# Coefficient transfers over every second partition, with another layout in DRAM

## The chip, the cores and the metric

The kernel runs on one core of one Trainium2 chip. The metric is device time in microseconds, the median of several executions. A profiled execution of the same kernel gives the profile; times in it count from the first instruction.

## The reference

The input x is an image batch of 4 x 64 channels x 256 x 256 in float32. Four layers follow each other. Layers 0, 2 and 3 are long two-dimensional convolutions whose filter is the outer product of two filters made by a small sine network, plus a scaled residual:

```python
k   = einsum('ijk,imk->ijmk', hx, hy)              # per channel: hx (rows) times hy (columns)
u_f = rfft2(x, s=(512, 512)); k_f = rfft2(k, s=(512, 512)) / 512
out = irfft2(u_f * k_f)[..., :256, :256] + x * bias[:, None, None]
```

Layer 1 works on Haar wavelet coefficients and mixes the channels at each coefficient:

```python
f1  = haar2d(x)
acc = 0
for i in range(2):                                  # two branches
    f4  = einsum('bchw,oc->bohw', f1 * v[i], conv_w[i])
    acc = acc + sign(f4) * relu(abs(f4) - tau[i])
y   = haar2d(acc, inverse=True) + x
```

The convolutions need whole images of one channel, the mixing needs all 64 channels of one coefficient. Between the two the data change their place, by way of DRAM.

## The kernel before

A convolution is two products with Toeplitz matrices (rows, then columns) on TensorE. The Toeplitz tiles tx and ty are read from DRAM with 64 rows of 1 KB a transfer. There are three phases. Phase A does layer 0 and the forward Haar transform, two channels by two images in a step. Phase B mixes the channels and applies the thresholds. Phase C does the inverse Haar transform and layers 2 and 3. The four images are two groups of two. B of group 0 runs beside the second half of A, B of group 1 beside the first half of C: each phase is a list of small pieces, and a helper interleaves two lists. All transfers are issued from the SP queue.

```python
P = 128;  B, C, N = 4, 64, 256
GROUPS = 2;  NB = B // GROUPS;  CI = 4 // NB        # 2 groups, 2 images, 2 channels a step
ROUNDS = C // CI                                    # 32 steps of A (and of C) in a group
STEPS = C                                           # 64 steps of B in a group
W = 2 * N                                           # two rows of coefficients

def coefficients(name):
    return dram.tile([STEPS // 2, 2, C, 2, NB, 2, N], F32, tag=name, name=name)
coef = [coefficients(f"coef{g}") for g in range(GROUPS)]     # A writes, B reads
mixed = [coefficients(f"mixed{g}") for g in range(GROUPS)]   # B writes, C reads
# ... cut ...
def half(r):
    return slice(r * ROW, (r + 1) * ROW)            # ROW = 64 partitions

def all_rows(grp_tile, c0, images):                 # the transfers of A's store and C's load
    n = 2 * NB * W                                  # 2048 elements, 8 KB
    pairs = []
    for e in range(CI):
        at = grp_tile.offset + (c0 + e) * n
        rows = bass.AP(grp_tile.tensor, at, [[2 * C * n, ROW // 2], [C * n, 2], [1, n]])
        pairs.append((rows, images[half(e)].rearrange("p n k -> p (n k)")))
    return pairs
```

In A and C partition e x 64 + m x 2 + q holds channel e of the step's two and pair of rows (m, q). One transfer takes one channel: 64 neighbouring partitions, 8 KB from each, to rows of DRAM that lie C x n = 131072 elements (512 KB) apart. A step has two such transfers.

```python
# phase A
def store(t):
    grp, c0 = t // ROUNDS, t % ROUNDS * CI
    for to, f in all_rows(coef[grp], c0, st[t]["f"]):
        nc.sync.dma_start(to, f)

# phase B: partition q * 64 + c holds channel c
def step_of(ap, s):
    n = NB * W                                      # 1024 elements, 4 KB
    return bass.AP(ap.tensor, ap.offset + (s // 2 * P * 2 + s % 2) * n, [[2 * n, P], [1, n]])

def load(s):
    # ... cut ...
    d["f"] = bp.tile([P, NB, W], F32, tag="ft", name=f"ft_{grp}_{s}", bufs=4)
    nc.sync.dma_start(d["f"].rearrange("p b w -> p (b w)"), step_of(coef[grp], s))
    for name, src in (("v", v), ("tau", taus)):     # 16 rows of DRAM, each to 8 partitions
        t = d[name] = bp.tile([P, 2, W], F32, tag=name, name=f"{name}_{grp}_{s}", bufs=3)
        at = src.offset + s * 4 * W * COPIES
        flat = bass.AP(src.tensor, at, [[2 * W, 2 * COPIES], [0, C // COPIES], [1, 2 * W]])
        nc.sync.dma_start(t.rearrange("p e w -> p (e w)"), flat)

def store(s):
    nc.sync.dma_start(step_of(mixed[grp], s), st[s]["g"].rearrange("p b w -> p (b w)"))

# phase C
def load(t):
    grp, c0 = t // ROUNDS, t % ROUNDS * CI
    st[t]["g"] = big("in", f"g_{t}", 3)
    for rows, g in all_rows(mixed[grp], c0, st[t]["g"]):
        nc.sync.dma_start(g, rows)
```

In B a step is one transfer of 128 partitions in each direction, 4 KB from each, at a pitch of 8 KB in DRAM. A step of B also loads v and tau. It multiplies the mixed channels by v (VectorE, line 602), takes sign and magnitude (ScalarE), subtracts tau and thresholds (VectorE), and adds up in gt (GpSimd). The load of step s+2 is issued in step s.

Of the kernel before, what the change touches and what calls it, by code (L numbers as in the profile page):

```python
# [41 lines left out]
F32 = mybir.dt.float32  # L42
# [5 lines left out]
P = 128  # L48
B, C, N = 4, 64, 256

ROW = 64
# [14 lines left out]
NB = B // GROUPS  # L66
CI = 4 // NB
M = CI * NB

ROUNDS = C // CI  # L70
STEPS = C
# [2 lines left out]
C_PIECES = 4 * BLOCKS + 2  # L74
W = 2 * N


IMAGES = (GROUPS, NB, ROUNDS, CI, BLOCKS, ROW, N)
TO_ROUNDS = (0, 2, 1, 5, 3, 4, 6)
# [10 lines left out]
def conv_haar_kernel(  # L90
    ctx: ExitStack, tc: tile.TileContext, x, zT, w1, wbd, cols, decay, wo_first, decay_first, bias, forward, inverse, wcol, wrow, pack, v, tau, out
):
    nc = tc.nc
# [3 lines left out]
    dram = ctx.enter_context(tc.tile_pool(name="dram", bufs=1, space=DRAM))  # L97


    def coefficients(name):  # L100
        return dram.tile([STEPS // 2, 2, C, 2, NB, 2, N], F32, tag=name, name=name)

    coef = [coefficients(f"coef{g}") for g in range(GROUPS)]
    mixed = [coefficients(f"mixed{g}") for g in range(GROUPS)]
# [22 lines left out]
    def load_x(t):  # L127
        grp, r = divmod(t, ROUNDS)
        xs = big("in", f"x_{t}", 3)

        n = BLOCKS if t == 0 else 2 * M
        for k in range(0, 2 * M, n):
            nc.sync.dma_start(xs[:, k : k + n], x[grp, r, :, k : k + n])
        return xs

    def load_toeplitz(l, t):

        tx = ac.tile([P, CI, N], F32, tag="tx", name=f"tx{l}_{t}", bufs=5)  # L140
        ty = ac.tile([P, N], F32, tag="ty", name=f"ty{l}_{t}", bufs=5)

        def rows(dst, w, e):
            start = (w * C + t % ROUNDS * CI + e) * REPEATS * PERIOD
            src = bass.AP(filt[l].tensor, filt[l].offset + start, [[PERIOD - 4, 16], [PERIOD - 1, 4], [1, N]])
            nc.sync.dma_start(dst, src)

        for e in range(CI):
            for r in range(2):
                rows(tx[r * ROW : (r + 1) * ROW, e, :], 0, e)  # L150
        for e in range(CI):
            rows(ty[e * ROW : (e + 1) * ROW, :], 1, e)
        return tx, ty
# [143 lines left out]
    def half(r):  # L297
        return slice(r * ROW, (r + 1) * ROW)
# [99 lines left out]
    def later(op):  # L398

        waiting.append(op)  # L400
# [8 lines left out]
        for _ in range(count):  # L409
            next(ops, None)  # L410

    def all_rows(grp_tile, c0, images):

        n = 2 * NB * W
        pairs = []
        for e in range(CI):
            at = grp_tile.offset + (c0 + e) * n
            rows = bass.AP(grp_tile.tensor, at, [[2 * C * n, ROW // 2], [C * n, 2], [1, n]])
            pairs.append((rows, images[half(e)].rearrange("p n k -> p (n k)")))
        return pairs  # L420

    def phase_a():


        total = GROUPS * ROUNDS
        st = [dict() for _ in range(total)]

        def filters(t):
            if t < total:
                st[t]["toep"] = first_toep[t] if t < FIRST else load_toeplitz(0, t)  # L430

        def load(t):
            if t < total:
                st[t]["x"] = first_x[t] if t < len(first_x) else load_x(t)

        def rows(t, j):
            s = st[t]
            if j == 0:
                s["y"] = big("t0", f"ay_{t}", 2)
            if j % 2 == 0:  # L440
                s["ps"] = banks(f"a1ps{j}_{t}")
            toeplitz(s["ps"], blocks(s["x"]), filters_x(s["toep"]), j)
            if j % 2:
                for r, ps in enumerate(s["ps"]):
                    y = blocks(s["y"])[:, r, j - 1 : j + 1]
                    later(lambda y=y, ps=ps: nc.scalar.copy(y, ps))

        def columns(t, j):
            s = st[t]
            if j == 0:  # L450
                s["x1"] = big("m0", f"x1_{t}", 2)
            if j % 2 == 0:
                s["ps2"] = banks(f"a2ps{j}_{t}")
            toeplitz(s["ps2"], blocks(s["y"]), filters_y(s["toep"]), j)
            if j % 2:
                for e, ps in enumerate(s["ps2"]):
                    later(lambda e=e, ps=ps: residual(t, e, j, ps))
            if j == BLOCKS - 1:
                s["fw"] = big("m1", f"fw_{t}", 2)
                s["ops"] = forward_free(s["x1"], s["fw"], f"f{t}_")  # L460

        def residual(t, e, j, ps):
            s = st[t]
            c = t % ROUNDS * CI + e
            to, old = (blocks(s[name])[:, e, j - 1 : j + 1] for name in ("x1", "x"))
            nc.vector.scalar_tensor_tensor(to, old, bias_sb[:, c : c + 1], ps, ALU.mult, ALU.add)  # L466

        def product(t, bp):
            s = st[t]
            if bp == 0:  # L470

                s["f"] = big("out", f"f_{t}", 2)
            two = banks(f"a3ps{bp}_{t}")
            fw = blocks(s["fw"])
            haar(two, lambda r, c: fw[half(r), c, 2 * bp : 2 * bp + 2], forward_sb)
            for b, ps in enumerate(two):
                f = s["f"][:, 4 * bp + 2 * b : 4 * bp + 2 * b + 2]
                copy = nc.vector.tensor_copy if b and t < ROUNDS else nc.scalar.copy
                later(lambda f=f, ps=ps, copy=copy: copy(f, ps))  # L479

        def store(t):
            grp, c0 = t // ROUNDS, t % ROUNDS * CI
            for to, f in all_rows(coef[grp], c0, st[t]["f"]):
                nc.sync.dma_start(to, f)
            st[t].clear()

        def piece(t, j):
            flush()
            if j == 0:
                if t == 0:  # L490
                    filters(0)
                    filters(1)
                    load(0)
                    load(1)
                    spread(0, 0)
                filters(t + 2)
            if j < BLOCKS:
                if t < total:
                    rows(t, j)
                if t > 1:  # L500
                    run(st[t - 2]["ops"], 3)
            elif j < 2 * BLOCKS:
                if 0 < t <= total:
                    columns(t - 1, j - BLOCKS)
                if j == BLOCKS and t > 2:
                    store(t - 3)
            else:
                if t > 1:
                    product(t - 2, j - 2 * BLOCKS)
                if 0 < t <= total:  # L510
                    run(st[t - 1]["ops"], 2)
                if j == 2 * BLOCKS + 1:
                    load(t + 2)

        pieces = [lambda t=t, j=j: piece(t, j) for t in range(total) for j in range(A_PIECES)]

        last = [lambda: [piece(total, j) for j in range(BLOCKS + 1)]]
        last += [lambda j=j: piece(total, j) for j in range(BLOCKS + 1, A_PIECES)]
        t = total - 1
        end = [lambda: (flush(), run(st[t]["ops"], 16), store(t - 1))]  # L520
        end += [lambda bp=bp: (flush(), product(t, bp)) for bp in range(2)]
        end.append(lambda: (flush(), store(t)))
        return pieces, last, end

    def phase_b(grp):
# [3 lines left out]
        st = [dict() for _ in range(STEPS)]  # L529
        un = [dict() for _ in range(units)]  # L530
        pieces = []

        def step_of(ap, s):
            n = NB * W
            return bass.AP(ap.tensor, ap.offset + (s // 2 * P * 2 + s % 2) * n, [[2 * n, P], [1, n]])

        def load(s):
            if s >= STEPS:
                return
            d = st[s]  # L540
            d["f"] = bp.tile([P, NB, W], F32, tag="ft", name=f"ft_{grp}_{s}", bufs=4)
            nc.sync.dma_start(d["f"].rearrange("p b w -> p (b w)"), step_of(coef[grp], s))
            for name, src in (("v", v), ("tau", taus)):
                t = d[name] = bp.tile([P, 2, W], F32, tag=name, name=f"{name}_{grp}_{s}", bufs=3)

# [3 lines that stand above are left out]
# [84 lines left out]
            un[u].clear()  # L633

        def store(s):
            nc.sync.dma_start(step_of(mixed[grp], s), st[s]["g"].rearrange("p b w -> p (b w)"))
            st[s].clear()

        def piece(u, j):
# [41 lines left out]
    def phase_c():  # L681
# [4 lines left out]
        st = [dict() for _ in range(total)]  # L686

        def load(t):
            if t >= total:
                return  # L690
            grp, c0 = t // ROUNDS, t % ROUNDS * CI
            st[t]["g"] = big("in", f"g_{t}", 3)
            for rows, g in all_rows(mixed[grp], c0, st[t]["g"]):
                nc.sync.dma_start(g, rows)

        def filters(t, l):
# [258 lines left out]
```

## Time and profile before

| what | value |
|---|---|
| time, median of 3 | 2965.0 us (2959.24 to 2973.0) |
| span of the profiled execution | 2974.9 us |
| TensorE matmul, weight load | 2459.2 us (83%), 1979.5 us (67%) |
| VectorE, ScalarE, GpSimd | 1583.0 us (53%), 1434.8 us (48%), 1946.2 us (65%) |
| moved by DMA | 636.23 MB, mean 214 GB/s |
| coef<-f, ft<-coef, mixed<-gt, g<-mixed | 128 transfers of 512 KB each |
| from issue to landing, median, in that order | 6.3, 11.1, 11.8, 8.8 us |
| v<-in_v, tau<-taus | 128 transfers of 512 KB each, 12.4 and 12.9 us |

How to read it: a share is an average over stages that have different limits, so the prediction takes the stages one by one. An arrow reads "written from": coef<-f is A's store, ft<-coef is B's load, mixed<-gt is B's store, g<-mixed is C's load, out<-o is the result. The span is also given in 40 equal slices with one digit each, the busy share in tenths. The DMA digit is the mean busy share of the core's 16 DMA engines, and GB/s is what they moved.

### The profile page before, as it was taken

To read this page: it belongs to the slowest core of one execution; us is meant where nothing else is said; L and a number is where in the kernel's file an instruction comes from. 1 tells how busy PE (TensorE), PEld (TensorE's weight loads), DVE (VectorE), ACT (ScalarE), POOL (GpSimd) and SP (SyncE) were. 2 spreads that over 40 slices of the span, in tenths; PEclk is the share of its full clock that TensorE was granted. 3 is DMA by queue.
4 is the path that set the end of the run, shared out by engine and by line. 5 is a ranking of instruction groups with operands and counts; after the bars stand their busy time and mean duration, and the time that the engine had idled before them with its cause. 6 is when DMAs were issued, how large, how long until landed. Compare 5 with 4: busy or idle time off the path is not lost.

```text
span 2974.9 us, 119229 instructions
## 1 busy us (share of the span) xinstructions
PE 2459.2 (83%) x53276; PEld 1979.5 (67%) x53276; DVE 1583.0 (53%) x1779; ACT 1434.8 (48%) x2361; POOL 1946.2 (65%) x2422
## 2 busy tenths in 40 slices
PE   6998887677777767768888888888879999999999
PEld 5777775444445445556767766666658887888888
DVE  2443335677777777446666666666652333333333
ACT  1222224566666666346666566666644333343332
POOL 2777766878778877647776776776755545555551
PEclk9999998888788888889999999999999999999999
DMA  5878888899999999677988898888856455454542
GB/s 164 229 213 234 236 244 229 233 270 293 284 267 290 287 280 290 172 194 221 253 243 241 245 249 242 240 242 236 243 167 161 121 141 136 130 146 122 152 126 92
DMA packets 219192, 636.23 MB, mean 214 GB/s; under 512 B 34983, under 2 KB 117576, under 8 KB 186169
## 3 DMA queue, kind: packets, MB, share of 16 engines
q1 hardware_dynamic: 218680, 628.61, 75.7%
q8 instruction: 419, 6.86, 1.0%
q14 instruction: 93, 0.75, 0.1%
HBM read 413.12 MB, written 215.35 MB: 211 GB/s over the span
## 4 chain that ended last, share of the span: by engine, by line
PE 48%; DMA 16%; issue 8%; DVE 6%; POOL 5%; ACT 4%; SPq 1%; DVEq 0%; ACTq 0%; POOLq 0%
PE c1c L304 10%; PE c1r L304 9%; PE c2c L304 9%; PE c2r L304 8%; PE f L587 4%; DMA ft<-coef 4%; DMA v<-in_v 4%; PE c0ps L316 3%; DMA mixed<-gt 2%; DVE x L602 2%; DMA x<-in_x 2%; PE a2ps L304 1%; POOL fw L352 1%; DMA tau<-taus 1%; PE a1ps L304 1%
## 5 line engine op out<-in xcount | busy, mean ns | idle before, releaser
L389 POOL TENSOR_TENSOR i<-i,g 128x16 f32<-128x16 f32 x744 | 393.9, 549 | 591.4 <-ACT g L372 572.3
L602 DVE TENSOR_TENSOR x<-f,v 128x1024 f32<-128x1024 f32 x256 | 312.6, 1221 | 344.1 <-PE f L587 275.9
L587 PE MATMUL f<-ft,mix 64*64 64x512 f32 x2048 | 357.1, 682 | 166.8 <-DMA ft<-coef 130.4
L606 ACT ACTIVATE m<-x 128x1024 f32<-128x1024 f32 x256 | 271.2, 1059 | 343.7 <-DVE x L602 256.1
L304 PEld LDWEIGHTS a1ps<-tx,x 64*64 64x64 f32 x8192 | 334.1, 143 | 134.2 <-ACT f L479 54.8
L304 PE MATMUL a1ps<-tx,x 64*64 64x192 f32 (+3 forms) x8192 | 367.9, 317 | 46.5 <-ACT f L479 23.4
L304 PE MATMUL c1r<-tx,z 64*64 64x192 f32 (+3 forms) x8192 | 337.4, 308 | 60.2 <-issue 60.1
L304 PEld LDWEIGHTS c1r<-tx,z 64*64 64x64 f32 x8192 | 313.5, 139 | 88.8 <-issue 69.4
L304 PE MATMUL c2r<-tx,cy 64*64 64x256 f32 (+3 forms) x8192 | 329.9, 303 | 50.4 <-issue 39.9
L304 PEld LDWEIGHTS c1c<-ty,ch 64*64 64x64 f32 x8192 | 313.5, 135 | 86.9 <-ACT z L723 41.5
L304 PEld LDWEIGHTS a2ps<-ty,ay 64*64 64x64 f32 x8192 | 311.1, 139 | 90.4 <-issue 51.4
L304 PE MATMUL a2ps<-ty,ay 64*64 64x128 f32 (+3 forms) x8192 | 343.2, 309 | 29.1 <-issue 21.9
L610 ACT ACTIVATE a<-x 128x1024 f32<-128x1024 f32 x256 | 264.2, 1032 | 211.5 <-DVE m L616 210.4
L304 PE MATMUL c2c<-ty,ch 64*64 64x128 f32 (+3 forms) x8192 | 332.5, 303 | 40.3 <-issue 37.1
L304 PE MATMUL c1c<-ty,ch 64*64 64x256 f32 (+3 forms) x8192 | 341.9, 302 | 26.2 <-issue 19.9
L304 PEld LDWEIGHTS c2r<-tx,cy 64*64 64x64 f32 x8192 | 309.4, 136 | 80.5 <-issue 53.5
L304 PEld LDWEIGHTS c2c<-ty,ch 64*64 64x64 f32 x8192 | 311.1, 136 | 65.9 <-issue 48.7
L613 DVE TENSOR_TENSOR a<-a,tau 128x1024 f32<-128x1024 f32 x256 | 313.9, 1226 | 41.2 <-ACT a L610 41.1
L735 ACT COPY ch<-c1r 128x512 f32<-128x512 f32 x256 | 137.2, 587 | 393.0 <-PE c1r L304 392.7
L466 DVE SCALAR_TENSOR_TENSOR x<-x,bias_sb,a2ps 128x512 f32<-128x512 f32 x256 | 179.6, 743 | 272.7 <-PE a2ps L304 232.9
L616 DVE SCALAR_TENSOR_TENSOR m<-a,m 128x1024 f32<-128x1024 f32 x256 | 313.2, 1223 | 21.7
L628 POOL TENSOR_TENSOR gt<-gt,m 128x1024 f32<-128x1024 f32 x128 | 302.9, 2366 | 19.9 <-DVE m L616 16.1
(71 smaller groups left out, 3228.5 us busy)
## 6 DMA issues: line engine op xcount, KB each, us to landing
coef<-f SPq DMA_DIRECT2D x128, 512.0 KB, 6.3
ft<-coef SPq DMA_DIRECT2D x128, 512.0 KB, 11.1
v<-in_v SPq DMA_DIRECT2D x128, 512.0 KB, 12.4
tau<-taus SPq DMA_DIRECT2D x128, 512.0 KB, 12.9
mixed<-gt SPq DMA_DIRECT2D x128, 512.0 KB, 11.8
g<-mixed SPq DMA_DIRECT2D x128, 512.0 KB, 8.8
x<-in_x SPq DMA_DIRECT2D x63, 1024.0 KB, 10.8
out<-o SPq DMA_DIRECT2D x63, 1024.0 KB, 4.9
```

What stands on the lines that cost most here:

```text
L304: nc.tensor.matmul(ps[r][half(c), j % 2, k * ROW :], data[half(r), c, k, bass.ts(j, ROW)], t(r, c)[:, : N - k * ROW], start=k == 0, stop=k ...
L316: nc.tensor.matmul(ps[r][half(c)].rearrange("p h k -> p (h k)"), matrix[half(r)], pairs(r, c).rearrange("p h k -> p (h k)"), start=True, s ...
L389: engine.tensor_tensor(to, s, d, op)
L466: nc.vector.scalar_tensor_tensor(to, old, bias_sb[:, c : c + 1], ps, ALU.mult, ALU.add)
L587: nc.tensor.matmul(un[u]["f4"][half(q), b, :], mixers[0][half(r), bass.ts(i, C)], st[s]["f"][half(r), b], start=True, stop=True, tile_posi ...
L602: nc.vector.tensor_tensor(un[u]["x"], un[u]["f4"], both(u, "v"), ALU.mult)
L606: nc.scalar.activation(un[u]["m"], un[u]["x"], AF.Sign)
L610: nc.scalar.activation(un[u]["a"], un[u]["x"], AF.Abs)
L613: nc.vector.tensor_tensor(un[u]["a"], un[u]["a"], both(u, "tau"), ALU.subtract)
L616: nc.vector.scalar_tensor_tensor(un[u]["m"], un[u]["a"], 0.0, un[u]["m"], ALU.max, ALU.mult)
L628: nc.gpsimd.tensor_tensor(st[s]["g"], st[s]["g"], m, ALU.add)
L735: later(lambda y=y, ps=ps: nc.scalar.copy(y, ps))
```

## The change

The four coefficient transfers are cut in another way, and the two DRAM tensors get another layout. The parity of the channel (e) becomes the outermost dimension of the tensor. Then come the 32 pairs of steps of B, each 2 x 32 rows of 8 KB plus one unused row of 8 KB: 133120 elements, 520 KB. In A and C a transfer takes one q, so it covers every second partition of all 128, and the pitch of its 64 rows in DRAM is 520 KB. In B a transfer takes one e, again every second partition. What was one transfer of 128 partitions is now two of 64. The aim is that a transfer of 64 partitions reaches into all of SBUF and not into one half, and that its rows in DRAM aren't a power of two apart. The bytes moved and all computation stay as they are.

```diff
+PAIR = 2 * ROUNDS * 2 * NB * W + 2 * NB * W
 ...
     def coefficients(name):
-        return dram.tile([STEPS // 2, 2, C, 2, NB, 2, N], F32, tag=name, name=name)
+        return dram.tile([CI, STEPS // 2, PAIR], F32, tag=name, name=name)
 ...
-    def all_rows(grp_tile, c0, images):
-
+    def all_rows(grp_tile, r, images):
+
+        by_q = images.rearrange("(m q) n k -> q m (n k)", q=2)
         n = 2 * NB * W
-        pairs = []
-        for e in range(CI):
-            at = grp_tile.offset + (c0 + e) * n
-            rows = bass.AP(grp_tile.tensor, at, [[2 * C * n, ROW // 2], [C * n, 2], [1, n]])
-            pairs.append((rows, images[half(e)].rearrange("p n k -> p (n k)")))
-        return pairs
+        at = [grp_tile.offset + (q * ROUNDS + r) * n for q in range(2)]
+        return [(bass.AP(grp_tile.tensor, at[q], [[PAIR, P // 2], [1, n]]), by_q[q]) for q in range(2)]
 ...
-        def step_of(ap, s):
+        def step_of(ap, s, images):
+
             n = NB * W
-            return bass.AP(ap.tensor, ap.offset + (s // 2 * P * 2 + s % 2) * n, [[2 * n, P], [1, n]])
+            by_e = images.rearrange("(m e) b w -> e m (b w)", e=CI)
+            at = [ap.offset + (e * STEPS // 2 + s // 2) * PAIR + s % 2 * n for e in range(CI)]
+            return [(bass.AP(ap.tensor, at[e], [[2 * n, P // CI], [1, n]]), by_e[e]) for e in range(CI)]
 ...
-            nc.sync.dma_start(d["f"].rearrange("p b w -> p (b w)"), step_of(coef[grp], s))
+            for rows, f in step_of(coef[grp], s, d["f"]):
+                nc.sync.dma_start(f, rows)
 ...
-            nc.sync.dma_start(step_of(mixed[grp], s), st[s]["g"].rearrange("p b w -> p (b w)"))
+            for to, g in step_of(mixed[grp], s, st[s]["g"]):
+                nc.sync.dma_start(to, g)
```

The callers of `all_rows` in A and C pass the step's number within the group instead of its first channel (cut here).

More of the change, by code (lines that the diff above doesn't have):

```diff
@@ L481, in store @@
         def store(t):
-            grp, c0 = t // ROUNDS, t % ROUNDS * CI
-            for to, f in all_rows(coef[grp], c0, st[t]["f"]):
+            for to, f in all_rows(coef[t // ROUNDS], t % ROUNDS, st[t]["f"]):
                 nc.sync.dma_start(to, f)
@@ L690, in load @@
                 return
-            grp, c0 = t // ROUNDS, t % ROUNDS * CI
             st[t]["g"] = big("in", f"g_{t}", 3)
-            for rows, g in all_rows(mixed[grp], c0, st[t]["g"]):
+            for rows, g in all_rows(mixed[t // ROUNDS], t % ROUNDS, st[t]["g"]):
                 nc.sync.dma_start(g, rows)
```

## The prediction

> **What bounds the kernel now.** I read the 40-slice view first, then the same counters over the stages that the code builds, then the waits of each stage, and last the single transfers that the change touches.
>
> ```profile
> PE   6998887677777767768888888888879999999999
> DMA  5878888899999999677988898888856455454542
> GB/s 164 229 213 234 236 244 229 233 270 293 284 267 290 287 280 290 172 194 221 253 243 241 245 249 242 240 242 236 243 167 161 121 141 136 130 146 122 152 126 92
> ```
>
> A slice is 74 us. Four stages show: phase A alone (to about 470 us), A beside B of image group 0 (480 to 1220), C beside B of group 1 (1300 to 2220), C alone. TensorE leads in the first and the last; in the second the DMA engines stand at 9 while TensorE is at 7. The busy times over the two middle stages say it in numbers:
>
> ```profile
> core 0: us, PE busy (x) PEld busy (x) DVE busy (x) ACT busy (x) POOL busy (x), PEclk, DMA share, GB/s
> 480.00:1220.00 740.00, 537.68 (x8564) 358.79 (x8568) 534.45 (x508) 449.54 (x604) 571.99 (x639) 0.84 0.94 274
> 1300.00:2220.00 920.00, 768.35 (x16426) 628.02 (x16428) 613.14 (x628) 585.21 (x934) 644.65 (x660) 0.95 0.85 233
> ```
>
> A+B: 740 us for about 63 steps of B, 11.7 us each; no engine over 77% (GpSimd), the DMA share 0.94. B+C: 14.6 us a step, TensorE 84%, DMA 0.85: neither fully bound. The waits of the A+B stage (engine, line, releaser: total us, times, longest) agree:
>
> ```profile
> PE f L587 <- DMA ft<-coef: 130.4, 41, 6.7
> DVE x L602 <- DMA v<-in_v: 51.4, 25, 4.6
> ```
>
> All 130 us in which the mixing matmuls wait for a coefficient load lie in A+B; in B+C this wait is absent from the list. So A+B is bound by its transfers, and engine time added to a transfer there is paid nearly in full.
>
> Now what a transfer costs by its shape. Short windows in which (by the trace's packet records: start, duration and bytes of each packet) almost only one kind of transfer moves:
>
> ```profile
> 2220.80:2222.10 1.30, 0.00 (x0) 0.00 (x0) 0.00 (x0) 0.00 (x0) 0.00 (x0) 1.00 0.98 403
> 2224.00:2228.50 4.50, 0.00 (x0) 0.00 (x0) 0.00 (x0) 0.00 (x0) 0.00 (x0) 0.59 1.02 232
> 233.00:236.40 3.40, 3.13 (x50) 1.77 (x48) 2.65 (x4) 1.17 (x2) 2.08 (x4) 1.00 1.01 230
> 480.60:482.40 1.80, 0.00 (x0) 0.00 (x0) 0.00 (x0) 0.00 (x0) 0.85 (x5) 0.50 1.03 218
> ```
>
> The last two columns are the share of the 16 DMA engines and the rate. In order: one B store of gt (128 partitions, one DMA), two C loads of g (64 neighbouring partitions each), A stores of coef (likewise 64), a B load of v (128 partitions from 16 source rows, each read 8 times). The engines are equally busy in all four, but the first moves 403 GB/s and the others 218 to 232. The packets say why: a 4 KB packet of that gt store takes 159 ns, an 8 KB packet undisturbed 309 ns, but those of g and of coef here 620 to 660 ns, twice that, and those of v mostly 250 to 330. A clean factor of two looks like two DMA engines sharing one entrance to SBUF.
>
> [...] Whether the 512 KB pitch hurts here, the trace doesn't separate directly; but a burst of tx loads from 2411.9 to 2412.6 us (64 partitions, no such pitch) also has 76 to 80 ns packets against 46 undisturbed. [...]
>
> **The change part by part.**
> 1. A stores and C loads keep two DMAs of 64 rows of 8 KB; the rows go to every second partition over all 128, and the DRAM pitch is 520 KB, not 512. [...] So I expect 8 KB packets near where they are when the queue starts from rest: phase A (mean of coef packets 527 ns) and C (g 548 ns) about unchanged, and TensorE leads there in any case.
> 2. B's load of ft and store of gt lose the one thing that worked: a 128-partition DMA becomes two of 64 partitions each, two apart. [...] I therefore price their packets like those of v and tau in the same stage. Means by stage: A+B ft 222, gt 182, v 282, tau 253 ns; B+C ft 204, gt 179, v 285, tau 258.
>    - A+B: (282+253)/2 = 268. An engine has 8 packets per DMA of 128 rows: (268-222)x8 + (268-182)x8 = 0.37 + 0.69 = 1.06 us a step.
>    - coef in A+B stands at 365 ns now[...] (72% of its packets take the bare 309). [...] I guess 430: 0.92 DMAs a step x 4 packets x 65 ns = 0.24 us.
>    - Sum 1.3 us on 11.7, paid in full: 63 x 1.3 = 82 us.
>    - B+C: (271-204)x8 + (271-179)x8 = 0.54 + 0.74 = 1.28 us a step; the engines are busy 0.85 x 14.6 = 12.4 us and come to 13.7 of 14.6. g stays near 556 ns. TensorE has 84% of the stage, so I let a third through: 0.43 x 63 = 27 us.
> 3. Issues: 128 more ft loads and 128 more gt stores, about 0.53 and 0.41 us each on the SP queue: 68 + 52 = 120 us in all. In A+B the SP issues fill 330 of 740 us now (492 issues), so some 60 more fit beside the rest. But SP signals completion through a ring of eight semaphores (each carries 269 or 270 DMAs), so at most about eight are under way: halving B's transfers shortens the backlog. With 10 us from issue to landing that is rather harmless.
> 4. Nothing computes differently; no other engine gains or loses an instruction.
>
> Sum: 82 + 27 = 109 us slower, 3074 us. I take about a quarter off, [...], and say **3045 us**.
>
> **Rivals.**
> - The pitch is the culprit[...]. For: coef and g, the slow ones, are just those with that pitch. Against: the exact doubling, v and tx, which have no such pitch and double too, and coef's 309 ns in A+B at the same pitch. If true, coef drops from 365 to 309: 0.2 us a step, 13 us in A+B; g from 556 to 309: 0.92 x 4 x 247 = 0.9 us a step of B+C, a third of it 19 us; a few us in A. With B's packets untouched: about 2930.
> - Every second partition really spreads the load [...]: A and C gain as above, and ft and gt stay near 160 to 200 ns. 2925 to 2960; it cannot be more, as ft and gt have nothing to win, v and tau are not touched, and C alone waits for TensorE.
> - The transfers get worse but the pace of a step is kept by GpSimd (77%) or the chain from mix to store: then A+B pays only part, about 2990 to 3010.
> - SP becomes the bound through its order: a half-size gt store waiting for GpSimd holds back the next loads. In B+C the store's waits for GpSimd are 71 us already. That would add 20 to 50 us, mostly in B+C.
>
> **Range and chances.** My theory and the third rival give 2990 to 3090, weight about 75%; the first two, 2925 to 2960, about 20%; the fourth adds at the top. Range 2945 to 3105. A gain over 2% means below 2906, beyond even the good rivals: 0.05. A loss over 2% means above 3024: 0.58. Within 2%: 0.37.
>
> **What would show each step right or wrong.** In the changed kernel: (a) a lone half store of gt or load of ft runs near 220 to 240 GB/s at full DMA share instead of 403: part 2 right; near 400: wrong, and with it the prediction. (b) A lone pair of g loads: near 230 GB/s[...]; near 400, one of the first two rivals. (c) The A+B stage grows from 740 towards 820 us at a DMA share still over 0.94, and the wait of the mixing matmul for ft grows from 130 us. (d) B+C grows by less than 40 us; A alone and C alone by under 10. (e) If the stages grow but the DMA share falls to 0.85 or less with longer SP waits, it was the fourth rival.

## The result, and the profile after

The changed kernel takes 2862.6 us (median of 4 runs, 2855 to 2867); the kernel before takes 2963.0 us. The ratio is 0.965, with a 95% interval of 0.962 to 0.969: 3.5% faster. The prediction was 3045 us, slower by 2.7%.

The page's 40-slice view of the changed kernel (a slice is 71 us):

```profile
PE   6999998676777777858888988888898999999999
DMA  5668778799999999756888888888874444444442
GB/s 154 221 216 259 236 272 248 218 284 284 279 292 280 279 290 266 253 189 194 252 258 242 254 270 241 267 259 259 256 227 157 142 148 154 137 158 132 161 129 93
```

The same four stages show. In phase A (slices 2 to 6) TensorE stays at 9 where it fell to 8, and in C alone (the last ten) the DMA row is mostly at 4 where it was at 4 and 5: the same bytes, moved in less engine time.

Stage lengths follow from four issue times, taken in the same way in every kernel here: the first ft load of group 0 (end of A), the last gt store of group 0 (end of A+B), the first ft load of group 1, the last gt store of group 1 (end of B+C).

| stage, us | before | after | difference |
|---|---|---|---|
| A alone | 471.2 | 456.8 | -14.4 |
| A+B | 744.5 | 743.7 | -0.8 |
| between | 71.5 | 65.7 | -5.8 |
| B+C | 932.8 | 884.6 | -48.2 |
| C alone | 754.8 | 706.8 | -48.0 |

So nothing was lost in A+B, where I had put 82 us. Most of the gain lies in B+C, where I had put a loss of 27 us, and in C alone, where I had put TensorE at its limit. Counters by stage in the changed kernel (columns as in the prediction), A+B, B+C and C alone:

```profile
core 0: us, PE busy (x) PEld busy (x) DVE busy (x) ACT busy (x) POOL busy (x), PEclk, DMA share, GB/s
470.00:1200.00 730.00, 537.39 (x8480) 355.29 (x8484) 530.26 (x501) 449.35 (x604) 567.30 (x622) 0.86 0.90 274
1275.00:2150.00 875.00, 757.67 (x16416) 623.14 (x16420) 611.14 (x628) 584.18 (x934) 645.43 (x660) 0.96 0.83 247
2150.00:2857.00 707.00, 678.37 (x18088) 618.90 (x18080) 238.29 (x340) 259.26 (x568) 364.22 (x513) 0.99 0.43 142
```

and C alone in the kernel before:

```profile
2220.00:2975.00 755.00, 696.24 (x18080) 624.27 (x18072) 238.45 (x340) 261.00 (x568) 363.84 (x512) 0.97 0.51 133
```

In A+B the DMA share fell from 0.94 to 0.90 and the stage did not get shorter. In C alone TensorE ran the same matmuls (18,080 and 18,088 of them in the records). It was idle for 29 us (707 - 678) where it had been idle for 59 (755 - 696), and at a granted clock of 0.99 instead of 0.97 it was busy for 18 us less. Why the clock rose is not shown.

**Single transfers.** Two short windows of the changed kernel, the first with two g loads alone, the second with two halves of a gt store:

```profile
2407.50:2409.00 1.50, 1.50 (x58) 1.48 (x54) 0.00 (x0) 0.95 (x2) 0.29 (x2) 1.00 1.01 404
2082.40:2083.60 1.20, 1.20 (x42) 1.16 (x38) 0.28 (x1) 1.20 (x3) 1.20 (x3) 1.00 1.02 403
```

Both move over 400 GB/s at full engine share. A pair of g loads moved 232 before; a gt store kept its 403, though it is now two DMAs over every second partition. The issue lists of the page say the same of the whole run, in us to landing: g had 8.8 before, ft is now twice as many transfers of half the size.

```profile
ft<-coef SPq DMA_DIRECT2D x256, 256.0 KB, 8.6
...
g<-mixed SPq DMA_DIRECT2D x128, 512.0 KB, 6.8
```

From the trace's packet records, the mean of one packet in ns (undisturbed: 159 for 4 KB, 309 for 8 KB):

| stage | transfer | before | after |
|---|---|---|---|
| A | coef (8 KB) | 527 | 325 |
| A+B | coef (8 KB) | 365 | 319 |
| A+B | ft / gt (4 KB) | 222 / 182 | 196 / 170 |
| A+B | v / tau (4 KB, not changed) | 282 / 253 | 281 / 247 |
| B+C | g (8 KB) | 556 | 367 |
| B+C | ft / gt | 204 / 179 | 200 / 173 |
| C alone | g (8 KB) | 548 | 334 |

**Where TensorE's time came from.** The waits of TensorE that no releaser explains are listed as "issue": nothing that the profile shows holds the engine, and it still does not start. The main ones in C alone, before and after (engine, line, releaser: total us, times, longest):

```profile
PE c2r L304 <- issue: 22.9, 11, 2.7
PE c1c L304 <- issue: 11.6, 12, 2.0
...
PE c0ps L316 <- issue: 8.2, 4, 2.8
```

```profile
PE c2r L307 <- issue: 11.7, 10, 1.8
...
PE c0ps L319 <- issue: 2.1, 3, 1.3
```

The same in B+C, before and after:

```profile
PE c1r L304 <- issue: 60.1, 25, 3.9
PE c2c L304 <- issue: 37.1, 22, 3.4
PE c2r L304 <- issue: 17.0, 15, 2.2
```

```profile
PE c1r L307 <- issue: 37.3, 24, 3.4
PE c2r L307 <- issue: 27.6, 16, 3.2
...
PE c2c L307 <- issue: 10.6, 11, 2.0
```

All such lines added: A 29.1 to 17.3, B+C 125.3 to 82.5, C alone 42.7 to 13.8 us. That is 84 of the 117 us by which the four stages and the gap between them became shorter. One step of C shows what it looks like. The chain that ended last in the kernel before has, from 2410.5 us on (start, length, what):

```profile
2410.52 2.07 PE c0ps L316 x14
2412.59 0.55 PE c1c L304 x9
2413.14 1.74 issue
2414.88 3.88 PE c1c L304 x82
```

and the same place in the changed kernel runs through:

```profile
2410.21 2.01 PE c0ps L319 x13
2412.22 4.25 PE c1c L307 x93
2416.47 0.15 PE c2c L307
```

What happens just ahead of the stop is in the DMA view of 2400 to 2450 us (slices of 1.25 us), before and then after:

```profile
DMA  0007989999722200400059999989332000030004
GB/s 3 0 13 315 419 223 262 216 224 178 203 68 49 68 3 0 95 23 0 13 216 413 229 321 210 210 167 236 91 86 49 0 0 13 0 83 22 13 0 210
...
q8 instruction: 9, 0.15, 1.3%
```

```profile
DMA  0019999973240022004998984341004000799988
GB/s 0 0 46 413 288 275 393 365 216 81 56 112 3 0 55 63 0 0 177 393 354 269 380 312 130 74 116 43 0 0 108 10 0 13 301 400 256 374 351 261
```

A step's store of out (1 MB), its g loads (1 MB) and the next filters leave as one burst. Before, the burst runs at 180 to 260 GB/s once out is through and fills the engines for some 10 us; after, at 270 to 390 GB/s but for its end, for some 8. Between the bursts stand the nine packets of queue q8, 0.15 MB in all: blocks of 16 KB, by their number (below) TensorE's own instructions. The packet records put their starts in the kernel before at 2402.98, 2412.11 and 2416.63: none starts for 9.1 us while the burst runs, and TensorE starts nothing from 2412.8 to 2414.9. The block was late before TensorE stopped, so it is not the stop that delayed the block. After, they start at 2405.63, 2410.20 and 2414.46, and TensorE does not stop there.

Queue q8, which the page lists as "instruction", moves 419 packets of 16 KB each in the whole run of either kernel, against 106,552 matmuls and weight loads: 254 each. That is why I take them for TensorE's instructions. In C alone after the change they are 142 for 36,168 matmuls and weight loads, 255 each, one per 5.0 us. TensorE stops for over 1 us, with few exceptions, only where a block starts over 6.8 us after the one ahead, so some 2 us late, as the counts under the table of the experiments show.

### The profile page after: what moved, and what is told of

It is laid out like the page before. It is cut to its first block, busy times and chain, and to the rows that moved or that the text cites. A ratio compares the mean times of both kernels' runs of the same rounds, so it can differ in the third digit from the quotient of the medians.

```text
span 2857.7 us, 119588 instructions
## 1 busy us (share of the span) xinstructions
PE 2433.7 (85%) x53276; PEld 1968.9 (69%) x53276; DVE 1580.6 (55%) x1779; ACT 1431.4 (50%) x2361; POOL 1948.1 (68%) x2422
## 4 chain that ended last, share of the span: by engine, by line
PE 43%; DMA 19%; DVE 7%; POOL 7%; issue 5%; ACT 4%; SPq 2%; DVEq 0%; ACTq 0%; POOLq 0%
PE c2r L307 9%; PE c1c L307 9%; PE c1r L307 8%; PE c2c L307 8%; DMA ft<-coef 5%; PE c0ps L319 4%; PE f L590 3%; DMA v<-in_v 3%; DMA x<-in_x 3%; DMA tau<-taus 2%; DMA coef<-f 2%; POOL fw L355 2%; DVE x L605 2%; POOL f L357 2%; DVE a L616 2%
## 5 line engine op out<-in xcount | busy, mean ns | idle before, releaser
L307 PE MATMUL a1ps<-tx,x 64*64 64x256 f32 (+3 forms) x8192 | 368.9, 316 | 45.5 <-ACT f L479 23.8
L307 PE MATMUL c2r<-tx,cy 64*64 64x192 f32 (+3 forms) x8192 | 342.9, 308 | 58.0 <-issue 39.3
L307 PEld LDWEIGHTS c2r<-tx,cy 64*64 64x64 f32 x8192 | 319.1, 139 | 88.0 <-issue 51.0
L307 PE MATMUL a2ps<-ty,ay 64*64 64x256 f32 (+3 forms) x8192 | 344.9, 309 | 20.2 <-ACT ay L446 10.3
L307 PE MATMUL c1c<-ty,ch 64*64 64x192 f32 (+3 forms) x8192 | 331.1, 300 | 6.9 <-ACT z L726 6.8
L307 PE MATMUL c2c<-ty,ch 64*64 64x256 f32 (+3 forms) x8192 | 320.6, 297 | 10.9 <-issue 10.6
L307 PEld LDWEIGHTS c2c<-ty,ch 64*64 64x64 f32 x8192 | 304.2, 133 | 29.4 <-issue 16.3
```

The source lines that it names most:

```text
L307: nc.tensor.matmul(ps[r][half(c), j % 2, k * ROW :], data[half(r), c, k, bass.ts(j, ROW)], t(r, c)[:, : N - k * ROW], start=k == 0, stop=k ...
```

## Experiments: the partitions or the pitch

The change does two things to the slow transfers: it spreads them over all 128 partitions, and it moves the DRAM rows from 512 KB apart to 520. Three kernels separate them.

**The spread without the pad.** The changed kernel at a pitch of 512 KB:

```diff
-PAIR = 2 * ROUNDS * 2 * NB * W + 2 * NB * W
+PAIR = 2 * ROUNDS * 2 * NB * W
```

> The changed kernel with the unused 8 KB row taken out, so every second partition but a DRAM pitch of 512 KB. Theory S (the spread over all of SBUF did it): g packets stay near 330 to 370 ns and coef near 320 ns, time 2850 to 2880 us. Theory P (the 512 KB pitch was the brake): g and coef packets go back to about 550 ns outside the A+B stage, C alone back to about 755 us from 707, time 2930 to 2980 us.

2875.0 us, ratio 0.9665 (0.963 to 0.970). coef packets in A 323 ns, g in C alone about 330: as fast as with the pad.

**The pad without the spread,** with B's transfers in halves of 64 neighbouring partitions:

```diff
-dram.tile([STEPS // 2, 2, C, 2, NB, 2, N], ...)
+dram.tile([STEPS // 2, 2, ROWS], ...)      # ROWS = C * 2 * NB * W + 2 * NB * W, 520 KB
-[[2 * C * n, ROW // 2], [C * n, 2], [1, n]]
+[[ROWS, ROW], [1, n]]
```

> The kernel before with a uniform DRAM pitch of 520 KB and A's and C's transfers still over 64 neighbouring partitions; B's transfers, too, become two of 64 neighbours each. Theory S: g and coef stay near 550 ns as in the kernel before, and B's ft and gt packets get worse as well (towards 250 to 320 ns from 180 to 220), so 2965 to 3060 us. Theory P: g and coef near 330 ns, ft and gt as before, 2860 to 2890 us.

3022.4 us, ratio 1.017 (1.014 to 1.020). coef 529 ns, g 556: still doubled. ft and gt, now over 64 neighbours, rose to 242 to 247 and 198 to 204 ns, and A+B to 773 us.

**The pad alone,** one per pair of steps, B's transfers whole as before:

```diff
-[[2 * C * n, ROW // 2], [C * n, 2], [1, n]]
+[[PAIR, ROW // 2], [C * n, 2], [1, n]]     # PAIR = 2 * C * n + n
```

> The kernel before with 8 KB unused after each pair of steps, so that the pitch is 512 KB within a pair of rows and 520 KB to the next; neighbours in A and C, B's transfers whole as before. Theory S: nothing changes, 2950 to 2980 us, g near 550 ns. Theory P: the rows of the engines no longer lie a power of two apart, g falls to 330 to 420 ns and the time to 2860 to 2900 us.

2970.2 us, ratio 1.001 (0.998 to 1.003). coef 532 ns, g 554.

The pitch does nothing measurable here; it is the partitions that make the packets fast. This disposes of the first rival.

**Fewer rows in a transfer.** A's stores and C's loads in four DMAs of 32 rows, first on 32 neighbouring partitions in the kernel before, then on every fourth partition in the changed kernel.

```diff
+for h in range(2):                          # before: two DMAs of 32 neighbours for one of 64
+    rows = bass.AP(..., at + h * (ROW // 4) * 2 * C * n, [[2 * C * n, ROW // 4], [C * n, 2], [1, n]])
```

```diff
-by_q = images.rearrange("(m q) n k -> q m (n k)", q=2)
+by_z = images.rearrange("(m z) n k -> z m (n k)", z=4)
```

> The kernel before with A's and C's transfers cut into quarters: four of 32 neighbouring partitions instead of two of 64. It asks how partitions share an entrance of SBUF. If eight neighbours share one (and an engine takes consecutive rows), 32 neighbours have 4 entrances for 16 engines and the 8 KB packets of lone transfers rise to about 1240 ns. [...] packets stay at 620 to 650 ns.

> The changed kernel with A's stores and C's loads in four DMAs of 32 rows on every fourth partition instead of two of 64 on every second. If rows are dealt to the engines as in a whole transfer, scaled to the number of rows, [...] a lone g packet takes 309 ns. If each engine got consecutive rows (as the prediction assumed), [...] a lone g packet would take 600 to 660 ns.

32 neighbours: lone packets mostly 620 to 660 ns, the same doubling, and not the 1240 that entrances of eight neighbours each would give (mean of g in C alone 546 ns, as with 64); 2918.1 us. Every fourth partition: lone packets 309 ns, mean in C alone 342; 2845.7 us. Each time is of one execution. So 32 neighbours are no slower from rest than 64, and every fourth partition no faster than every second. The prediction assumed that an engine takes consecutive rows and that pairs of engines then meet in spread transfers too, with packets of 600 to 660 ns. They take 309 ns, so the assumption as a whole is wrong. Which engine takes which row, and which partitions share an entrance, the trace does not show.

## Experiments: B's transfers in halves

The changed kernel with ft and gt as one DMA of 128 rows each; the rows in DRAM are those of the change:

```diff
-return [(bass.AP(ap.tensor, at[e], [[2 * n, P // CI], [1, n]]), by_e[e]) for e in range(CI)]
+rows = bass.AP(ap.tensor, at, [[2 * n, P // CI], [STEPS // 2 * PAIR, CI], [1, n]])
+return [(rows, images.rearrange("p b w -> p (b w)"))]
```

> The changed kernel with B's load and store as one transfer of 128 partitions each again, taking the two parities in turn, from the new layout. It undoes the halving in B and leaves A and C changed. If the row order inside a transfer decides [...], ft and gt packets rise to 250 to 290 ns and the time to 2880 to 2940 us. If the halving in B only cost issues, packets stay at 170 to 200 ns and the time is 2845 to 2865 us.

2848.8 us, ratio 0.960 (0.956 to 0.964), against 0.965 (0.962 to 0.969) for the change: the intervals just meet. The stage is clearer: A+B takes 720.9 us, and 737 to 750 in the five kernels with the spread and B in halves (one profile each; that of 720.9 is of the fastest execution, 2835.6 us). ft packets are no faster than in halves (209 to 212 ns). The waits of A+B in the changed kernel show the loss:

```profile
PE f L590 <- DMA ft<-coef: 91.9, 33, 6.6
...
DVE x L605 <- DMA v<-in_v: 66.6, 30, 4.3
```

The mixing matmuls wait for ft less than before (130 us), but VectorE waits for v more (51 before), and with whole DMAs it waits for v only this much:

```profile
DVE x L605 <- DMA v<-in_v: 35.0, 21, 4.5
```

The halves give back in A+B what the faster packets bring. Since SP's own waits for DMA completions fall with halves (338 us before, 270 after, by the sum of its list for A+B), I take it that fewer bytes are under way: in both kernels at most eight DMAs of SP are under way at once, by the issues and landings in the trace. This was not tried by itself.

## Experiments: what TensorE gained

The theory: a block of instructions that falls due during a burst starts only when the burst has drained, and what matters is for how long the engines are filled. The rival: the doubled packets themselves cost time, at SBUF or by g's late arrival.

**g ahead of out,** in the kernel before:

```diff
                 filters(t, 2)
-            if j == 2 * BLOCKS and t + 3 != alone:
-                load(t + 3)
+                if t + 3 != alone:
+                    load(t + 3)
```

> The kernel before with one thing moved: C issues its g load right behind the filter loads, ahead of the store of the result, instead of after it. Transfers and packets stay slow (g about 550 ns). If C alone lost time because the filter loads tx and ty queue up behind two slow g loads just when TensorE needs them, C alone falls from 755 us towards 705 to 720 us and the time to 2880 to 2930 us. If C alone was bound by TensorE or by the rate of the transfers, nothing changes: 750 us, 2955 to 2980 us.

2937.5 us, ratio 0.988 (0.984 to 0.992); C alone 734.3 us, with g packets at 573 ns. That lies between the two expectations: something of C alone comes back though the packets stay slow. The g loads moved in all of C here, and B+C became 11 us shorter too.

**g between the row and the column filters** in C alone, again in the kernel before, so that out and g leave in two bursts:

```diff
-                filters(t, 2)
-            if j == 2 * BLOCKS and t + 3 != alone:
+                filters(t, 2, (lambda: load(t + 3)) if t >= alone else None)   # issued between tx and ty
+            if j == 2 * BLOCKS and t + 3 != alone and not (t >= alone):
```

> The kernel before with its slow transfers untouched; only the place of the g loads in C alone moves: behind the row filters tx of the same step, ahead of its column filters ty, so that out (1 MB) and g (1 MB) no longer arrive at the DMA engines in one burst. Theory (TensorE's instruction fetches stand behind the burst): g packets stay near 550 ns, yet the idle time of TensorE on 'issue' in C alone falls from 36 us to 12 to 18, C alone from 755 to 705 to 725 us, the whole to 2915 to 2940. Rival (the doubled packets themselves cost C alone its 48 us, by conflicts at SBUF or by late g): C alone stays at 748 to 757, the whole at 2960 to 2970.

2947.4 us, ratio 0.9935 (0.992 to 0.995); C alone 736.9 us with g at 570 ns. The rival fails: g is as slow as ever and C gains 18 us. But I had expected 30 to 50. (The profile is of an execution at 2959.0 us, 12 above the median.)

**1 MB more, then 3 MB more, in a step of C alone,** in the changed kernel, from DRAM to DRAM behind g:

```diff
                 load(t + 3)
+                if alone <= t < total:
+                    for k in range(3):              # the first of the two runs has one copy
+                        to = dram.tile([P, 2 * M, N], F32, tag=f"spare{t}_{k}", name=f"spare_{t}_{k}")
+                        nc.sync.dma_start(to, x[(t + k) % GROUPS, t % ROUNDS])
```

> The changed kernel with 1 MB more to move in each step of C alone (a copy from DRAM to DRAM that nobody reads, behind the g loads, 32 times; no SBUF partition is touched). Theory (fetches behind the burst): g packets stay fast, but the burst is 4 us longer or more, so the gaps between fetches and the idle time of TensorE on 'issue' come back: from 13 us to 30 or more, C alone from 707 to 735 to 780 us, the whole to 2890 to 2935. Rival (doubled packets at SBUF are what counted): C alone 705 to 715, the whole 2858 to 2872.

> The changed kernel with 3 MB more to move in each step of C alone (copies from DRAM to DRAM, no SBUF partition touched), where 1 MB more had cost 12 us over 32 steps. Theory (instruction packets stand behind the data): [...] intervals between instruction packets of 11 to 14 us, C alone 770 to 860 us, nearly all of the growth idle time on 'issue'. Rival (the gaps only go along with slow g packets): C alone stays below 730. If TensorE waits for tx or ty loads instead, the waits name a DMA.

1 MB: 2869.2 us, ratio 0.967 (0.963 to 0.971), not to be told from the change itself; C alone 718.7 us, 12 more, much less than expected. 3 MB: 2972.7 us, ratio 1.004 (1.001 to 1.007): the whole gain of the change is gone. C alone is 832.1 us, though g still takes 332 ns a packet. TensorE's waits there:

```profile
PE c1c L307 <- issue: 48.4, 26, 3.4
PE c2c L307 <- issue: 30.9, 14, 3.6
PE c2r L307 <- issue: 14.4, 13, 2.1
PE c2r L307 <- ACT ch L738: 8.5, 1, 8.5
```

No wait names a tx or ty load. The growth of 125 us is 97 us of gaps between TensorE's starts, as the table below shows, and a longer busy time at a lower granted clock, as the counters of the stage show (721 us busy instead of 678, clock 0.96):

```profile
2150.00:2975.00 825.00, 721.30 (x18064) 642.57 (x18064) 238.32 (x340) 259.49 (x568) 362.57 (x512) 0.96 0.69 242
```

**No out at all** in the kernel before, for the second image group (half of the result is left out):

```diff
-            if t < total - 1:
+            if t < alone:
                 nc.sync.dma_start(out[t // ROUNDS, t % ROUNDS], st[t]["y"])
```

> The kernel before without the stores of out for the second image group (the last image of it excepted), so half of the result is left out; g packets keep their neighbouring partitions and stay near 550 ns. Theory: the burst in C alone shrinks from 2 MB to 1 MB and the intervals above 8 us (18 of 141) vanish; idle time on 'issue' from 43 to under 20 us, C alone 695 to 715 us. Rival (the doubled packets themselves cost the time): C alone 745 to 757.

2946.0 us, ratio 0.994 (0.990 to 0.999). C alone 739.5 us: 15 gained, where 40 to 60 were expected. So the bytes in the burst are not the measure: at 91 GB/s this kernel moved two thirds of the bytes of the changed kernel's C (142 GB/s in 707 us), and TensorE has 29 us of "issue" waits against 14 there:

```profile
PE c1r L304 <- issue: 14.5, 9, 2.6
PE c2r L304 <- ACT ch L735: 10.3, 1, 10.3
PE c2r L304 <- issue: 9.7, 11, 1.5
PE c0ps L316 <- issue: 3.4, 1, 3.4
```

The following is worked out from the packet records and TensorE's starts in C alone: the intervals from the start of one instruction block to the next, for how long 14 or more DMA engines moved data within such an interval ("full"), and the gap of over 0.45 us from one TensorE start to the next about its end. "All" is the whole of C alone. A wait for ScalarE of 8.4 to 10.4 us at the start of the stage, which every kernel has, and the end of the program are left out of the gaps.

```
                          5 to 6.8 us               over 6.8 us               all              C alone
                          number  full    gap       number  full    gap       full    gaps     us
before                      22    3.1     0.23        27    6.7     1.81      325     58.1     754.8
g between filters           24    2.4     0.23        26    3.5     1.35      273     40.5     736.9
no out                      38    1.5     0.08        19    5.0     1.88      220     39.0     739.5
after                       21    3.4     0.07        19    5.3     0.92      238     19.6     706.8
after, 1 MB more            18    4.3     0.18        25    6.1     1.05      323     32.5     718.7
after, 3 MB more            25    4.3     0.98        45    7.3     1.96      508    116.6     832.1
every fourth partition      41    3.3     0.08         5    4.2     1.29      227     10.2     698.8
32 neighbours               28    4.5     0.36        17    5.8     0.83      319     24.1     711.7
```

The first half of the theory holds. Before, 20 of TensorE's 22 gaps of over 1 us follow an interval of over 6.8 us, and those 20 end 2.6 to 3.0 us after the late block's start; after, all 10 do, at 2.3 to 2.7 us. With 3 MB of data more, which touch neither SBUF nor g's speed, the late blocks and the gaps come back. In C alone the gaps shrank by 38.5 us of the 48.0 that the stage gained. The rest goes with the clock: C alone less the gaps is 696 to 701 us in the first three rows (clock 0.97 to 0.98), 686 to 689 in the four rows at 0.99, and 716 with 3 MB (0.96).

The second half fails. The engines are full for 325 us before, for 323 with 1 MB more and for 319 with 32 neighbours, and the gaps are 58, 33 and 24 us. Over the intervals the correlation of length and full time is 0.90 before and 0.84 after, but 0.61 with g between the filters. Neither bytes nor full time says how late a block will be, and the two misses stay unexplained. In the four kernels that differ only in the coefficient transfers, the gaps follow the time for which one g transfer holds an engine. If the 64 packets of a transfer fall evenly on the 16 engines, four to each, that is, as an estimate from the mean packets of g, 4 x 0.55 = 2.2 us before (58 us of gaps), 2 x 0.55 = 1.1 with 32 neighbours (24), 4 x 0.33 = 1.3 after (20) and 2 x 0.34 = 0.7 with every fourth partition (10). No run was made to test this.

B+C was not tested by itself. There too, 48 of the 52 "issue" waits of over 1 us before follow an interval of over 6.8 us. But over the runs these waits and the length of the stage don't go together: 125 us of waits in 933 before, 83 in 885 after, 124 in 927 with 32 neighbours, 68 in 954 with the pad and 64 neighbours, 40 in 892 with every fourth partition. So its 43 us of fewer waits are an account and not a shown cause.

What stays open: what makes a block late in one burst and not in another, and why gaps of 40 us remain with g and out apart.

## Experiments: the rows that are read eight times, and a better version

v and tau are each read from 16 DRAM rows, every row for 8 partitions. Two kernels with the spread and B's transfers whole: v laid out in 64 copies so that no row is read twice; and v and tau with their rows kept, but each in two DMAs over every second partition.

```diff
-"v": f(np.repeat(v[:, :, None], COPIES, axis=2)),
+"v": f(np.repeat(v[:, :, None], C, axis=2)),
 # and in the load, for v alone:
-flat = bass.AP(src.tensor, at, [[2 * W, 2 * COPIES], [0, C // COPIES], [1, 2 * W]])
+flat = bass.AP(src.tensor, at, [[2 * W, 2 * C], [1, 2 * W]])
```

```diff
-nc.sync.dma_start(t.rearrange("p e w -> p (e w)"), flat)
+parts = t.rearrange("(m z) e w -> z m (e w)", z=2)      # flat with C // COPIES // 2 repeats
+for z in range(2):
+    nc.sync.dma_start(parts[z], flat)
```

> The changed kernel with B's transfers whole again, and v given in DRAM with 64 copies instead of 8, so that each of the 128 partitions reads a row of its own. The bytes moved in the kernel are the same. If reading one row eight times is what makes v's packets slow (280 ns), they fall to 160 to 210 ns and the time to 2800 to 2835 us; tau, unchanged, stays at 250 ns. If their slowness is on the SBUF side, v stays at 270 to 290 ns and the time at 2840 to 2860 us.

> The changed kernel with B's transfers whole again, and v and tau each loaded in two transfers over every second partition, from the same rows. If v and tau are slow because neighbours meet at an entrance of SBUF[...], their packets fall from 250 to 285 ns to 160 to 190 ns and the time to 2790 to 2840 us. If they are slow on the DRAM side (one row read many times), packets stay at 240 to 290 ns, and two more transfers a step cost as the halving of ft and gt did: 2855 to 2885 us.

64 copies: 2800.1 us, ratio 0.9415 (0.939 to 0.945); v falls from 281 to 217 ns in A+B and 198 in B+C, A+B to 707 us. Every second partition: 2802.8 us, ratio 0.943 (0.939 to 0.947); v 250, tau 224 ns, A+B 701 us. So v's neighbouring partitions are part of its slowness. With 64 copies more of it goes, but that kernel changes two things: no row is read twice, and the transfer is 128 rows at one pitch instead of 16 rows eight times. Which of the two counts is not separated. In the second kernel halving the DMAs cost less than it brought.

Both together, with tau over every second partition and g between the filters; then also coefficients over every fourth partition:

> The changed kernel with B's ft and gt in one DMA each, v given in 64 copies (no row read twice), tau in two DMAs over every second partition, and the g loads between row and column filters in all of C. If the gains add: v alone brought 2849 to 2800; tau's packets should fall from 260 to near 225 ns (8 packets a step, 0.25 us a step of A+B and less of B+C: some 15 us together), and C gains up to 10 us as its idle time on 'issue' is only 13 us now. 2775 to 2795. If halved DMAs cost what they gain: 2800 again.

> Everything of the run with all together, and A's stores and C's loads in four DMAs of 32 rows on every fourth partition, which alone had brought C from 707 to 699 us. If both gains in C are the same one, 2770 to 2780; if they add, 2760 to 2770.

2777.3 us, ratio 0.937 (0.934 to 0.940), and 2762.1 us, ratio 0.932 (0.929 to 0.936): the best version, 3.4% below the changed kernel by the ratios. C alone takes 700.0 and 697.5 us, so the two gains there are nearly the same one; the quarters shorten B+C more, from 866 to 853 us. In the first of the two kernels the mixing matmul waits 0.6 us for ft in all of A+B, which takes 692 us:

```profile
PE a3ps L321 <- DVE x L468: 45.3, 24, 12.1
PE a2ps L309 <- ACT ay L448: 37.4, 37, 2.8
...
PE f L601 <- DMA ft<-coef: 0.6, 1, 0.6
```

TensorE now waits for the other engines there, and the stage is no longer held by its transfers.

## Why the prediction was wrong, point by point

- **Part 1, packets that stay doubled in the spread transfers:** wrong, and the first failing step. Lone spread packets take 309 ns; the means are 325 for coef in A and 334 for g in C alone. That engines meet there as well was the author's assumption and is shown by no trace, and it carried the sign of the whole prediction. The doubling does go with neighbouring partitions (g 556 ns at a pitch of 520 KB); that two engines then share one entrance to SBUF was the author's picture of it, and no record shows an entrance. The second rival had the outcome.
- **Part 2, B's transfers get v's pattern:** wrong from the same step, and from taking v as the model. The term of 82 us in A+B measured -0.8. ft and gt became slightly faster; v was no model for them: its 282 ns fall to 217 when every partition has a row of its own. The prediction had this difference in view ("each read 8 times") and did not weigh it.
- **"Engine time in A+B is paid nearly in full":** too strong. The share fell from 0.94 to 0.90 at the same length. Faster v did shorten the stage (707 us with 64 copies, 720.9 without), so it did hang on its loads; the busy share of the DMA engines did not say by how much.
- **Part 3, halving "rather harmless":** about 23 us in A+B (720.9 against 743.7), by one profile each.
- **"TensorE leads in A and C alone in any case":** the second failing step, and the costlier one for the rivals. TensorE was busy 92% of C alone, and of its 59 idle us 43 were "issue" waits, listed in the profile of before and not weighed. C alone gained 48 us where under 10 of change were expected. B+C's 27 us to lose became 48 to gain; its "issue" waits fell by 43 us, but what shortened that stage is not shown.
- **Rivals.** The pitch: refuted by three runs. The spread by itself: right on every packet, but its 2925 to 2960 rested on "C alone waits for TensorE". GpSimd and SP order: not seen; SP's waits for GpSimd in B+C fell.
- **The signs.** (a) and (b) came out against the theory: 403 and 404 GB/s. (c) and (d) failed in the direction of a gain; (e) did not arise.

## What to carry to other kernels

When a transfer takes less than 128 partitions, take every second or every fourth of them rather than neighbours: here it brought the 8 KB packets of g in C alone from 548 ns to 334 with 64 rows in one DMA and to 342 with 32. An engine that "leads" at 92% can still give something (here 43 of its 59 idle us were "issue" waits, and 14 were left): look at what its idle time is put down to before calling a stage its own. If it is "issue" on an engine with many short instructions, look at when its instruction blocks arrive and at what the DMA engines carry just then. Neither the bytes of a burst nor the time for which it fills the DMA engines told here how late a block would come; the starts of the blocks did.

## What the runs showed of the hardware

- TensorE stops when its next 16 KB of instructions come late: at 5.0 us of work per block, 20 of its 22 gaps of over 1 us in C alone before follow an interval of over 6.8 us between two blocks, and those end 2.6 to 3.0 us after the late block's start. Not every such interval stops it (19 of them and 10 gaps after). Instruction blocks are 1% of the DMA engines' time; the gaps in C alone come to 58 us of 755 before and 20 of 707 after.
- Lone transfers of 64 rows on every second and of 32 rows on every fourth partition run at the undisturbed 309 ns per 8 KB; 64 and 32 neighbours mostly take 620 to 660.
- v, with each DRAM row read by eight partitions of one transfer, takes 281 ns per 4 KB packet; with a row for each partition, and the transfer described as 128 rows, 217 in A+B and 198 in B+C.
- Row pitches of 512 and 520 KB do not differ (323 and 325 ns for coef).
